# A graph network's edge lists, counts and first projections put in another order on one core

## The chip, the core and the metric

The kernel runs on one core of a Trainium2 chip. Five engines work side by side, each through its own instructions in order, and meet through semaphores: TensorE (PE; matrix products into PSUM), VectorE (DVE), ScalarE (ACT), GpSimd (POOL) and SyncE (SP, which only issues transfers and waits). Transfers are issued by SyncE, ScalarE and GpSimd. The metric is the time of the whole program on the device in microseconds (us).

## The reference

N = 1250 nodes with 768 features, 41,250 edges sorted by target. A normalized copy of x goes through two graph attention layers, the result is added to x, and a transformer block with attention and a mixture of eight experts follows. What the change touches lies before and in the first graph layer:

```python
def _gat_layer(x, W, a_src, a_dst, b, src, dst, n_nodes):
    h = x @ W
    e_src = h @ a_src
    e_dst = h @ a_dst
    e = leaky_relu(e_src[src] + e_dst[dst], 0.2)
    m = segment_max(e, dst, num_segments=n_nodes)
    w = exp(e - m[dst])
    z = segment_sum(w, dst, num_segments=n_nodes)
    alpha = w / z[dst]
    return segment_sum(h[src] * alpha[:, None], dst, num_segments=n_nodes) + b

# first layer, on layernorm(x); loops appended to the edges
h = _gat_layer(x, W1, att_src1, att_dst1, b1, src, dst, n_nodes)
```

The kernel has no gather of h by edge. It turns the edges into a matrix of counts, cnt (how often source j meets target i), and then the layer is dense: weights from outer sums and exponentials, times the counts, times h.

## The kernel before

Nodes are cut into ten tiles of 125 (T = 125, NT = 10). The stretch up to the first aggregation has these steps.

**Edge lists (lines 226 to 390).** The edges are read as 125 rows of 330, and each becomes one number, key = target * 1250 + source (L234). The keys go back to DRAM. VectorE compares the rows' first keys with the nodes (L288), TensorE sums that (L292), and so each pair of nodes knows the row in which its edges begin. Five gathers by GpSimd fetch those rows (kr, L329), VectorE counts in them (`first_edges`, L299) and five more gathers fetch the 128 keys from each pair's first edge on (win, L302). L353 to L366 take the pair's base off, throw out what isn't the pair's and sum what was found; L380 transposes the lists, and L385 to L390 split each into a part of the target and source (pb, jb). If not all edges were found, a slow loop at L413 counts them by another way: `turns` is 0 when all were found, and then it runs no turn.

**Row tiles.** For each tile of x, `spread` takes mean and deviation (L120 to L124), `normal` normalizes the rows (L317, ScalarE), `columns` transposes them into xT (L141, copied by L273), and `project` multiplies a tile with W1 (gw) into h: 12 products, each shown as two matmuls, 24 a tile (L204), then one copy (L207).

**Tables.** GpSimd writes `lane` (128 x 3200) and `upto` (128 x 2500) with iotas (L250, L332).

**Counts (L392 to L407).** In 25 groups VectorE builds one-hot tables, oh in each group (L400) and ohj in every fifth (L397), TensorE makes 25 small products from them (L404), and ScalarE copies the sums into cnt (L406). oh and the PSUM tile pc have two buffers each.

**After the loop at L413.** The diagonal is added (L433), VectorE multiplies W1 with the attention vectors (reps; `attention_vector`, L182), TensorE makes the terms (L194) and es (L473), VectorE the maxima (L480 to L501), and `rest_of_first` (L535) projects the tiles from EARLY on. Weight tiles wt (L517) and h meet in the aggregation (L524).

**What sets the order.** Inside `tc.manual_schedule` the order of the program text is the order of the named engines: TensorE, VectorE and GpSimd from L323 on, TensorE and VectorE in the counts. `tc.keep_in_program_order` does so for single instructions, here the loads and stores of SyncE and ScalarE. All else is ordered by a planner, within a block of code; a loop such as L413 ends a block, and nothing moves past it. A transfer holds one of a few semaphores, and a later one that gets the same semaphore is issued only when the earlier has landed.

Of the kernel before, what the change touches and what calls it, by code (L numbers as in the profile page):

```python
# [10 lines left out]
F32 = mybir.dt.float32  # L11
F16 = mybir.dt.float16
BF16 = mybir.dt.bfloat16
I32 = mybir.dt.int32
# [3 lines left out]
ALU = mybir.AluOpType  # L18
# [9 lines left out]
def gnn_ffn_kernel(  # L28
# [132 lines left out]
    with tc.tile_pool(name="cnt", bufs=1) as cpool:  # L161
# [36 lines left out]

        def project(xT, w, h, psum, tiles):
            for t in tiles:  # L200
                po = psum.tile([T, 2, 512], F32, tag="po", name="ph")
                for s in range(2):
                    for c in range(DC):
                        nc.tensor.matmul(po[:, s, :DH], xT[:, c, t * T:(t + 1) * T],  # L204
                                         w[:, c, s * DH:(s + 1) * DH],
                                         start=(c == 0), stop=(c == DC - 1))
                nc.scalar.copy(h[:, t, :D].rearrange("p (s d) -> p s d", s=2), po[:, :, :DH])  # L207
# [6 lines left out]
        EARLY = 3  # L214
        with tc.tile_pool(name="edge", bufs=1) as ep, \
# [4 lines left out]
            def queue(eng, o, i):  # L220

                for rs in (slice(0, 112), slice(112, T)):
                    tc.keep_in_program_order(eng.dma_start(o[rs], i[rs]))
# [5 lines left out]
            for i, (eng, a) in enumerate(((nc.sync, dst), (nc.scalar, src))):  # L229
                queue(eng, ri[:, i, :], a.rearrange("(p e) -> p e", p=T))  # L230
            tc.keep_in_program_order(nc.scalar.dma_start(keys[E:E + SL].rearrange("(o e) -> o e", o=1), tail))
# [12 lines left out]
            nc.vector.tensor_scalar(pair, pair, 2.0 * N, None, ALU.mult)  # L244
            nodes = ep.tile([T, N], F32, name="nodes")
# [4 lines left out]
            nc.gpsimd.iota(lane, pattern=[[1, P], [0, PG]], base=0, channel_multiplier=0,  # L250
                           allow_small_or_imprecise_dtypes=True)
# [23 lines left out]

            with tc.tile_pool(name="early", bufs=1) as xp:
                xrows = [xp.tile([T, D], F32, name=f"xn{t}") for t in range(NT)]
                krows = [xp.tile([T, EC], F32, name=f"kr{u}") for u in range(NU)]
                queue(nc.scalar, xrows[1], x[T:2 * T, :])
                queue(nc.scalar, rows, key)  # L280
                for t in (0, 2, 3):
                    queue(nc.sync, xrows[t], x[t * T:(t + 1) * T, :])
                tc.keep_in_program_order(nc.sync.dma_start(gw, gW1.rearrange("(c p) f -> p c f", p=P)))
                for t in range(4, NT):
                    queue(nc.sync, xrows[t], x[t * T:(t + 1) * T, :])
# [22 lines left out]
                def spread(t):  # L308
                    stats[t] = ln_root(xrows[t])
# [9 lines left out]
                def columns(t):  # L319
                    transpose_rows(gpt, xrows[t], evict_to(xT, t))  # L320

                fixed = {mybir.EngineType.PE, mybir.EngineType.DVE, mybir.EngineType.Pool}
                with tc.manual_schedule(engines=fixed):  # L323
                    pk = find_rows()
                    spread(0)
                    nc.vector.tensor_scalar(row, pk[:T, :NU], -1.0, None, ALU.add)
                    nc.vector.tensor_scalar(edges, pk[:T, :NU], -1.0, float(EC), ALU.add, ALU.mult)
                    for u in range(NU):
                        nc.gpsimd.indirect_dma_start(  # L329
                            out=krows[u], out_offset=None, in_=rows,  # L330
                            in_offset=bass.IndirectOffsetOnAxis(ap=row[:, u:u + 1], axis=0))
                    nc.gpsimd.iota(upto, pattern=[[1, 2 * NT], [0, 5 * PG]], base=1, channel_multiplier=0,  # L332
                                   allow_small_or_imprecise_dtypes=True)
                    for t in range(1, 4):
                        spread(t)
                        normal(t - 1)
                        columns(t - 1)
                    normal(3)
                    columns(3)

                    for t in range(4, NT):
                        if t < 4 + NU:
                            first_edges(t - 4)
                        spread(t)
                        if t > 4:
                            normal(t - 1)
                        if t % 2 == 0:
                            project(xT, gw, h, gpo, [t // 2 - 2])
                        if t > 4:
                            columns(t - 1)  # L350
                    normal(NT - 1)
                    columns(NT - 1)
                    nc.vector.tensor_tensor(win, win, pair[:, :, None].to_broadcast([T, NU, SL]), ALU.subtract)  # L353

            op = edge.enter_context(tc.tile_pool(name="onehot", bufs=2))
            reps = [every_partition(a, op, "rep", nc.sync) for a in (ga_src1, ga_dst1)]

            wf = win.rearrange("p u s -> p (u s)")
            ge = ep.tile([T, NU * SL], F32, name="ge")
            nc.vector.tensor_scalar(ge, wf, 0.0, None, ALU.is_ge)  # L360
            found = ep.tile([T, 1], F32, name="found")
            nc.vector.scalar_tensor_tensor(ge, wf, 2.0 * N, ge, op0=ALU.is_lt, op1=ALU.mult,
                                           accum_out=found)
            FAR = 1048576.0
            nc.vector.scalar_tensor_tensor(wf, wf, FAR, ge, op0=ALU.add, op1=ALU.mult)
            nc.vector.tensor_scalar(wf, wf, -FAR, None, ALU.add)  # L366
            pf = gpt.tile([P, 4, P], F32, tag="tr", name="psum")
            nc.tensor.matmul(pf[:, 0, 0:1], ones[:T, :P], found, start=True, stop=True)
            good = ep.tile([P, 1], F32, name="good")
            nc.vector.tensor_scalar(good, pf[:, 0, 0:1], float(E), None, ALU.is_equal)  # L370
            turns = ep.tile([1, 1], I32, name="turns")
            nc.vector.tensor_scalar(turns, good[0:1], -float(EC // EB), float(EC // EB), ALU.mult, ALU.add)


            lt = op.tile([P, NP], F32, name="lt", bufs=1)
            for u0 in range(0, NU, 4):
                n = min(4, NU - u0)
                pt = gpt.tile([P, 4, P], F32, tag="tr", name="pl")
                for u in range(u0, u0 + n):
                    nc.tensor.transpose(pt[:, u - u0, :T], win[:, u, :], ident[:T, :T])  # L380
                nc.scalar.copy(lt[:, u0 * T:(u0 + n) * T].rearrange("p (u q) -> p u q", q=T), pt[:, :n, :T])

            jf = op.tile([P, NP], F32, name="jf", bufs=1)
            half = (T - 1) // 2
            nc.vector.tensor_scalar(jf, lt, -float(half), 1.0 / T, ALU.add, ALU.mult)  # L385
            nc.vector.tensor_scalar(jf, jf, 12582912.0, -12582912.0, ALU.add, ALU.add)
            pb = ep.tile([P, NP], BF16, name="pb")
            nc.vector.scalar_tensor_tensor(pb, jf, -float(T), lt, op0=ALU.mult, op1=ALU.add)
            jb = ep.tile([P, NP], BF16, name="jb")
            nc.vector.tensor_scalar(jb, jf, 1.0, good, ALU.add, ALU.mult)  # L390
            ohj = op.tile([P, NP // (5 * PG), 2 * NT, 5 * PG], BF16, name="ohj", bufs=1)
            with tc.manual_schedule(engines={mybir.EngineType.PE, mybir.EngineType.DVE}):  # L392
                for g in range(NP // PG):
                    gs = slice(g * PG, (g + 1) * PG)
                    if g % 5 == 0:
                        js = slice(g * PG, (g + 5) * PG)
                        nc.vector.tensor_tensor(ohj[:, g // 5], jb[:, None, js].to_broadcast([P, 2 * NT, 5 * PG]), upto,  # L397
                                                ALU.is_equal)
                    oh = op.tile([P, P, PG], BF16, tag="oh", name="ohp")
                    nc.vector.tensor_tensor(oh, pb[:, None, gs].to_broadcast([P, P, PG]), lane, ALU.is_equal)  # L400
                    pf = epc.tile([P, 512], F32, tag="pc", name="pc")
                    pc = pf[:, :PG * 2 * NT].rearrange("p (q e) -> p q e", e=2 * NT)
                    for k in range(PG):
                        nc.tensor.matmul(pc[:, k, :], oh[:, :, k], ohj[:, g // 5, :, (g % 5) * PG + k], start=True, stop=True)  # L404
                    c0 = 2 * g * PG
                    nc.scalar.copy(cnt[:, :, c0:c0 + 2 * PG],  # L406
                                   pc[:T].rearrange("p q (i j) -> p j (q i)", i=2))  # L407
# [23 lines left out]
            for t in range(NT):  # L431
                d = cnt[:, t, t * T:(t + 1) * T]
                nc.vector.tensor_tensor(d, d, ident[:T, :T], ALU.add)  # L433
            for i, a in enumerate(reps):
                attention_vector(0, i, gw, a, op, "scr")
# [656 lines left out]
```

## Time and profile before

| | us |
|---|---|
| median of 3 runs (lowest, highest) | 1527.41 (1524.62, 1529.33) |
| the profiled execution | 1522.34 |
| its span | 1520.5 |
| first key gather issued (L329) | 10.54 |
| weights gw landed, first projection starts (L204) | 19.32 |
| lists' transposes (L380) | 52.01 |
| first and last matmul of the counts (L404) | 59.26 to 112.11 |
| diagonal (L433) | 113.20 |
| es copied, maxima begin (L482) | 132.25 |
| first aggregation matmul (L524) | 190.20 |

All the change is in the first 190 us. Busy time of TensorE over the span is 1433.7 us, of VectorE 811.9, of ScalarE 595.6, of GpSimd 418.6. The page counts an engine as busy while an instruction of it is in flight, so a full TensorE may still run at half its clock; the granted clock is a column of its own. To find what a change in one stage is worth, one looks for the engine that ends each wait in that stage.

### The profile page before, as it was taken

The page shows a single profiled execution, that of the slowest core. Times are in us where ns is not written, and L with a number is a line of the kernel's source. Part 1 is how long each engine was busy: PE and PEld are TensorE (multiplying, and loading weights), DVE is VectorE, ACT ScalarE, POOL GpSimd, SP SyncE. Part 2 cuts the span into 40 slices and gives each one's busy share as a digit, 9 for nine tenths or more (in the row PEclk, how much of TensorE's full clock was granted, in tenths as well). Part 3 has the DMA queues.
Part 4 walks back from the last instruction along what each step waited for, and adds up shares of the span by engine and source line. Part 5 has one row for each costly group of instructions (what it writes and reads, how often), then busy time and mean ns, then how long its engine had stood idle before and what let it go on. Part 6 is the DMA issues. An engine that isn't in the chain of part 4 may idle for free.

```text
span 1520.5 us, 15858 instructions
## 1 busy us (share of the span) xinstructions
PE 1433.7 (94%) x5952; PEld 779.0 (51%) x5952; DVE 811.9 (53%) x1311; ACT 595.6 (39%) x924; POOL 418.6 (28%) x276
## 2 busy tenths in 40 slices
PE   6787999999999999999999999999989996899997
PEld 4574555556555555543343343344333664565654
DVE  6688456434036640127778778778787764111111
ACT  4221513205116521136556646646656354221211
POOL 5000000000000010006646646655657222122222
PEclk9758999999999999999999999999999997899999
DMA  7000020010021139920000000000120432855643
GB/s 207 22 2 11 11 73 0 0 32 1 15 88 45 57 100 396 407 86 0 22 1 0 22 1 21 1 22 0 28 75 1 144 119 107 300 172 185 219 153 134
DMA packets 48199, 124.66 MB, mean 82 GB/s; under 512 B 5629, under 2 KB 22207, under 8 KB 48120
## 3 DMA queue, kind: packets, MB, share of 16 engines
q1 hardware_dynamic: 31468, 57.36, 11.5%
q0 software_dynamic: 11968, 56.26, 9.8%
q10 hardware_dynamic: 4684, 9.99, 2.2%
q8 instruction: 48, 0.79, 0.2%
q14 instruction: 31, 0.25, 0.1%
HBM read 70.47 MB, written 57.60 MB: 84 GB/s over the span
## 4 chain that ended last, share of the span: by engine, by line
PE 67%; DVE 9%; issue 7%; ACT 4%; DMA 4%; POOL 1%; POOLq 0%; SPq 0%; ACTq 0%; DVEq 0%
PE pagg L524 13%; PE st L676 8%; PE ph L204 7%; PE pav L720 7%; PE pk L639 5%; PE pv L655 5%; PE phe L1006 5%; PE poe L1015 5%; PE pq L639 4%; DMA xd<-yn,slot 2%; DVE sT L706 2%; PE po L864 2%; ACT sT L679 1%; DVE most L685 1%; PE mb L701 1%
## 5 line engine op out<-in xcount | busy, mean ns | idle before, releaser
L712 POOL TENSOR_TENSOR acc<-acc,sT 125x834 f32<-125x834 f32 (+1 forms) x139 | 273.1, 1964 | 10.9
L524 PE MATMUL pagg<-h,wt 125*125 125x385 f32 (+1 forms) x800 | 263.5, 486 | 0.4 <-DVE wt L517 0.4
L685 DVE TENSOR_TENSOR most<-most,st 125x834 f32<-125x834 f32 (+1 forms) x144 | 147.0, 1021 | 105.5 <-ACT sT L679 102.6
L524 PEld LDWEIGHTS pagg<-h,wt 125*125 125x125 f32 x800 | 147.0, 187 | 104.7 <-DVE wt L517 3.5
L706 DVE TENSOR_TENSOR sT<-sT,mb 125x834 f32<-125x834 f32 (+1 forms) x180 | 174.1, 1015 | 22.6 <-PE mb L701 22.6
L707 ACT ACTIVATE sT<-sT 125x834 f32<-125x834 f32 (+1 forms) x180 | 158.4, 900 | 49.2 <-DVE sT L706 48.8
L679 ACT COPY sT<-st 125x834 f32<-125x834 f32 (+1 forms) x180 | 151.6, 848 | 52.4 <-PE st L676 50.7
L676 PE MATMUL st<-qk 64*125 64x417 f32 (+1 forms) x720 | 164.5, 556 | 3.9 <-DVE most L685 3.8
L720 PE MATMUL pav<-sT,v 125*64 125x417 f32 (+1 forms) x720 | 151.0, 532 | 9.0 <-ACT sT L707 9.0
L617 POOL MEMSET zero<- 128x772 f32 x1 | 0.7, 742 | 530.2 <-PE ptr L141 530.2
L712 POOL TENSOR_TENSOR acc<-sT 125x834 f32<-125x834 f32 (+1 forms) x18 | 35.4, 1965 | 274.6 <-ACT sT L707 274.6
L676 PEld LDWEIGHTS st<-qk 64*125 64x125 f32 x720 | 56.5, 184 | 99.1 <-issue 42.7
L720 PEld LDWEIGHTS pav<-sT,v 125*64 125x64 f32 x720 | 42.5, 136 | 105.7 <-issue 43.9
L1015 PE MATMUL poe<-we,hT 128*128 128x384 f32 x264 | 88.8, 486 | 0.0
L639 PE MATMUL pq<-yT,wqk 128*128 128x417 f32 (+1 forms) x216 | 88.1, 534 | 0.0
L864 PE MATMUL po<-wp,aT 128*125 128x384 f32 x240 | 87.5, 498 | 0.0
L1019 DVE SCALAR_TENSOR_TENSOR sofar<-poe,weight,sofar 128x768 f32<-128x768 f32 x25 | 25.4, 1018 | 114.6 <-PE poe L1015 107.7
L1006 PE MATMUL phe<-xT,we 128*128 128x384 f32 (+1 forms) x288 | 86.6, 460 | 0.0
L639 PE MATMUL pk<-yT,wqk 128*128 128x417 f32 (+1 forms) x216 | 84.0, 526 | 0.0
L204 PE MATMUL ph<-gw,xnT 128*125 128x384 f32 x240 | 81.4, 498 | 0.5 <-DMA gw<-in_L_gnn_W_dram 0.5
L655 PE MATMUL pv<-wv,yT 128*125 128x384 f32 x240 | 79.9, 490 | 1.4 <-issue 1.4
L528 DVE RECIPROCAL rz<-pagg 125x1 f32<-125x1 f32 x20 | 3.3, 166 | 141.5 <-PE pagg L524 141.5
(222 smaller groups left out, 1788.2 us busy)
## 6 DMA issues: line engine op xcount, KB each, us to landing
xd<-zero POOLq DMA_DIRECT2D x8, 3860.0 KB, 15.2
we<-in_L_ffn_W_dram SPq DMA_DIRECT2D x16, 1152.0 KB
xr<-xd SPq DMA_DIRECT2D x25, 386.0 KB
gw<-in_L_gnn_W_dram SPq DMA_DIRECT2D x2, 2304.0 KB
wqk<-in_L_ffn_Wqkv_dram SPq DMA_DIRECT2D x12, 384.0 KB
xres<-in_x_dram SPq DMA_DIRECT2D x10, 375.0 KB
xsd<-xres ACTq DMA_DIRECT2D x10, 375.0 KB
xn<-in_x_dram SPq DMA_DIRECT2D x9, 336.0 KB
```

The costliest lines, as they stand in the source:

```text
L204: nc.tensor.matmul(po[:, s, :DH], xT[:, c, t * T:(t + 1) * T], w[:, c, s * DH:(s + 1) * DH], start=(c == 0), stop=(c == DC - 1))
L524: nc.tensor.matmul(po[:, s, :DH + s], ws[j][:, (d - d0) * T:(d - d0 + 1) * T], h[:, j, s * DH:(s + 1) * DH + s], start=(j == 0), stop=(j = ...
L639: nc.tensor.matmul(pq[:, :w], wqk[:, c, i, :], yT[:, c, c0:c0 + w], start=(c == 0), stop=(c == DC - 1))
L676: nc.tensor.matmul(st[:T, i, :w], self.qk[r, 1, j * T:(j + 1) * T], self.qk[r, 0, self.c0:self.c0 + w], start=True, stop=True)
L679: nc.scalar.copy(s[:, :, :w], st[:T, :, :w])
L685: nc.vector.tensor_tensor(self.most[:, :, :w], prev[:, :, :w], st[:T, :, :w], ALU.max)
L706: nc.vector.tensor_tensor(s[:, :, :w], s[:, :, :w], self.mb[:T, :, :w], ALU.subtract)
L707: nc.scalar.activation(s[:, :, :w], s[:, :, :w], AF.Exp)
L712: nc.gpsimd.tensor_tensor(self.acc[:, :, :w], prev[:, :, :w], s[:, :, :w], ALU.add)
L720: nc.tensor.matmul(self.pav[r, :w], v[:, j, hd0:hd0 + HD], s[:, i, :w], start=(j == 0), stop=(j == NT - 1))
L1006: nc.tensor.matmul(ph[:, :n * P], w1[:, c, f * P:(f + 1) * P], xT[:, c, :n * P], start=(c == 0), stop=(c == DC - 1))
L1015: nc.tensor.matmul(po[:, d, :DH], hT[:, f, s * P:(s + 1) * P], w2[:, f, d * DH:(d + 1) * DH], start=(f == 0), stop=(f == FC - 1))
```

## The change

It moves work rather than taking it away:

- The tables lane and upto are no longer written by GpSimd. GpSimd writes one row table, upto128, and ScalarE copies it out, lane at the start and upto after the columns of tile 3.
- The store of the keys and of their tail, before on ScalarE's queue, is on SyncE's, between the rows of tile 0 and those of tiles 2 and 3.
- The rows of tiles 4 to 9 are loaded straight into h's space, and wait for the last of the five key gathers.
- All five `first_edges` come before the statistics of tile 4. The list steps come ahead of the statistics of tiles 7, 8 and 9.
- Tile 0 is projected before the columns of tile 4, tile 1 behind the lists' transposes, tile 2 one product at a time within the counts (groups 9 to 23, three of four), tiles 3 and 4 behind the counts but before the loop at L413. EARLY goes from 3 to 5, so five tiles are left after es instead of seven.
- Normals and columns of tiles 8 and 9 and the statistics of tile 9 lie within the counts; ohj has two buffers of one fifth each.
- The attention rows (reps) are loaded after the loop and the diagonal instead of before.

```diff
+        def project_steps(xT, w, h, psum, t):
+            po = psum.tile([T, 2, 512], F32, tag="po", name="ph")
+            for s in range(2):
+                for c in range(DC):
+                    nc.tensor.matmul(po[:, s, :DH], xT[:, c, t * T:(t + 1) * T],
+                                     w[:, c, s * DH:(s + 1) * DH],
+                                     start=(c == 0), stop=(c == DC - 1))
+                    if s == 1 and c == DC - 1:
+                        nc.scalar.copy(h[:, t, :D].rearrange("p (s d) -> p s d", s=2), po[:, :, :DH])
+                    yield None
+
         def project(xT, w, h, psum, tiles):
             for t in tiles:
...
+                for _ in project_steps(xT, w, h, psum, t):
+                    pass
...
-        EARLY = 3
+        EARLY = 5
...
-            tc.keep_in_program_order(nc.scalar.dma_start(keys[E:E + SL].rearrange("(o e) -> o e", o=1), tail))
...
+            upto128 = ep.tile([P, P + 1], F32, name="upto128")
+            nc.gpsimd.iota(upto128, pattern=[[1, P + 1]], base=0, channel_multiplier=0,
+                           allow_small_or_imprecise_dtypes=True)
...
-            nc.gpsimd.iota(lane, pattern=[[1, P], [0, PG]], base=0, channel_multiplier=0,
-                           allow_small_or_imprecise_dtypes=True)
...
+                xrows = [xp.tile([T, D], F32, name=f"xn{t}") if t < 4 else h[:, t, :D] for t in range(NT)]
                 krows = [xp.tile([T, EC], F32, name=f"kr{u}") for u in range(NU)]
                 queue(nc.scalar, xrows[1], x[T:2 * T, :])
-                queue(nc.scalar, rows, key)
-                for t in (0, 2, 3):
+                tc.keep_in_program_order(nc.scalar.copy(lane, upto128[:, :P, None].to_broadcast([P, P, PG])))
+                queue(nc.sync, xrows[0], x[0:T, :])
+                queue(nc.sync, rows, key)
+                tc.keep_in_program_order(nc.sync.dma_start(keys[E:E + SL].rearrange("(o e) -> o e", o=1), tail))
+                for t in (2, 3):
                     queue(nc.sync, xrows[t], x[t * T:(t + 1) * T, :])
                 tc.keep_in_program_order(nc.sync.dma_start(gw, gW1.rearrange("(c p) f -> p c f", p=P)))
-                for t in range(4, NT):
-                    queue(nc.sync, xrows[t], x[t * T:(t + 1) * T, :])
...
                     for u in range(NU):
-                        nc.gpsimd.indirect_dma_start(
+                        ins = nc.gpsimd.indirect_dma_start(
                             out=krows[u], out_offset=None, in_=rows,
                             in_offset=bass.IndirectOffsetOnAxis(ap=row[:, u:u + 1], axis=0))
-                    nc.gpsimd.iota(upto, pattern=[[1, 2 * NT], [0, 5 * PG]], base=1, channel_multiplier=0,
-                                   allow_small_or_imprecise_dtypes=True)
+
+                    for t in range(4, NT):
+                        for load in queue(nc.sync, xrows[t], x[t * T:(t + 1) * T, :]):
+                            if t == 4:
+                                tc.add_manual_dep(load.ins, ins.ins.name, mybir.DependencyInfo(
+                                    mybir.DependencyClass.Sync, mybir.DependencyReason.DATA), reason="rows of edges first")
...
                     normal(3)
                     columns(3)
-
-                    for t in range(4, NT):
-                        if t < 4 + NU:
-                            first_edges(t - 4)
+                    tc.keep_in_program_order(nc.scalar.copy(
+                        upto, upto128[:, 1:2 * NT + 1, None].to_broadcast([P, 2 * NT, 5 * PG])))
+                    for u in range(NU):
+                        first_edges(u)
+                    project(xT, gw, h, gpo, [0])
+                    for t in range(4, 7):
                         spread(t)
                         if t > 4:
                             normal(t - 1)
-                        if t % 2 == 0:
-                            project(xT, gw, h, gpo, [t // 2 - 2])
-                        if t > 4:
                             columns(t - 1)
-                    normal(NT - 1)
-                    columns(NT - 1)
+                    normal(6)
+                    columns(6)
+
                     nc.vector.tensor_tensor(win, win, pair[:, :, None].to_broadcast([T, NU, SL]), ALU.subtract)
-
-            op = edge.enter_context(tc.tile_pool(name="onehot", bufs=2))
-            reps = [every_partition(a, op, "rep", nc.sync) for a in (ga_src1, ga_dst1)]
...
+                    nc.vector.scalar_tensor_tensor(wf, wf, FAR, ge, op0=ALU.add, op1=ALU.mult)
+                    nc.vector.tensor_scalar(wf, wf, -FAR, None, ALU.add)
+                    pf = gpt.tile([P, 4, P], F32, tag="tr", name="psum")
+                    nc.tensor.matmul(pf[:, 0, 0:1], ones[:T, :P], found, start=True, stop=True)
+
+                    for u0 in range(0, NU, 4):
+                        n = min(4, NU - u0)
+                        pt = gpt.tile([P, 4, P], F32, tag="tr", name="pl")
...
+                    spread(7)
+                    nc.vector.tensor_scalar(good, pf[:, 0, 0:1], float(E), None, ALU.is_equal)
...
+                    nc.vector.tensor_scalar(jb, jf, 1.0, good, ALU.add, ALU.mult)
+                    spread(8)
+                    normal(7)
+                    project(xT, gw, h, gpo, [1])
+                    columns(7)
+                    more = project_steps(xT, gw, h, gpo, 2)
+                    for g in range(NP // PG):
...
+                        nc.vector.tensor_tensor(oh, pb[:, None, gs].to_broadcast([P, P, PG]), lane, ALU.is_equal)
+                        if g in (2, 3):
+                            normal(g + 6)
+                        if g == 2:
+                            spread(9)
+                        if g in (4, 6):
+                            columns(g // 2 + 6)
+                        if g > 7 and g % 4 != 0:
+                            next(more)
...
+                    for _ in more:
+                        pass
+                    project(xT, gw, h, gpo, range(3, EARLY))
...
             for t in range(NT):
                 d = cnt[:, t, t * T:(t + 1) * T]
                 nc.vector.tensor_tensor(d, d, ident[:T, :T], ALU.add)
+            reps = [every_partition(a, op, "rep", nc.sync) for a in (ga_src1, ga_dst1)]
```

## The prediction

> **What bounds the kernel now.** I first looked at the busy shares: TensorE is busy for 94% of the span, but in the first tenth the granted clock is low. The change touches only the stretch up to the first aggregation matmul at 190.20 us, so I read that stretch in order of time (start, busy us, engine, line, operation, count, idle time before it and who ended it):
>
> ```profile
> 10.54 1.38 POOL L329 DMA_INDIRECT kr<-keys,row  x1 [2.62 <-DVE st L120]
> 18.65 0.56 DVE L299 SCALAR_TENSOR_TENSOR key<-kr,pair,ones 125x330 f32<-125x330 f32 x1 [4.33 <-DMA kr<-keys,row]
> 19.32 10.54 PE L204 MATMUL ph<-gw,xnT 128*125 128x384 f32 x24 [0.51 <-DMA gw<-in_L_gnn_W_dram]
> ...
> 34.83 0.83 DVE L353 TENSOR_TENSOR win<-win,pair 125x640 f32<-125x640 f32 x1 [0.38 <-DMA win<-keys,at]
> ...
> 40.26 7.91 PE L204 MATMUL ph<-gw,xnT 128*125 128x384 f32 x24
> 52.01 0.75 PE L380 MATMUL pl<-ident,win 125*128 125x125 f32 x5
> 59.26 3.64 PE L404 MATMUL pc<-ohj,ohp 128*128 128x20 bf16 x50 [6.49 <-DVE ohp L400]
> ```
>
> The lists (win) are finished by VectorE at 38.4, yet their transposes (L380) run at 52.01: they stand behind the second and third projected tile on TensorE. Counting starts at 59.25 and its last matmul ends at 112.11, 52.85 us later. In that stage VectorE sets the pace: five one-hot tables take 9.54 us, 1.91 each, and every fifth group adds 1.46 for ohj, while TensorE needs 1.82 a group. The windows view (busy us of each engine, then the granted clock) says at what clock:
>
> ```profile
> core 0: us, PE busy (x) PEld busy (x) DVE busy (x) ACT busy (x) POOL busy (x), PEclk, DMA share, GB/s
> 60.00:112.00 52.00, 44.82 (x617) 42.97 (x615) 48.74 (x28) 13.87 (x24) 0.00 (x0) 0.50 0.01 2
> ```
>
> Then comes the guarded loop at L413, which runs no turn. The view of that line and the chain of waits show that it is a meeting of all engines:
>
> ```profile
> L413 SPq EVENT_SEMAPHORE  x12: 28/28/54886, 53.6 to 112.8; - x12
> L413 POOLq EVENT_SEMAPHORE  x12: 42/43/55061, 53.3 to 112.9; - x12
> ```
>
> ```profile
> 112.13 0.48 ACT cnt L406
> 112.61 0.03 DVEq L413
> ...
> 113.20 2.08 DVE cnt L433 x10
> 115.28 6.17 DVE scr L182 x14
> ```
>
> SyncE and GpSimd have nothing to do with the counts, and wait 55 us there until the last count has been copied. VectorE goes through only after ScalarE's last copy. So whatever stands before L413 on TensorE or ScalarE holds VectorE's next work. After it, the diagonal, the attention vectors and terms take 19.0 us up to the terms es (132.2), and from there TensorE is full with seven projected tiles until 190.0. The tenth weight tile wt is ready at 171.4.
>
> **The change, part by part.**
>
> *Lists, up to the first count matmul: before 59.25.* The two tables leave GpSimd. The five-element operation on pair took 2.47 us and ended with the lane table; now begun ends near 6.2 instead of 8.27. The row numbers then wait for x rows and their statistics (1.2 us), and the gather also stood behind the next tile's statistics (1.1 us): first gather about 9.3 instead of 10.54. ScalarE copies instead: its activations cost 0.96 us per 1000 elements plus 0.23 (500 in 0.71, 375 in 0.59 us), so lane 3.3 us and upto 2.6 us. I put both at nothing: lane runs about 4.4 to 7.7, before the first root (9.46 before), and upto while ScalarE waits for rows; without that cover they cost their 3.3 and 2.6. The key store and the tail move to SyncE, where tiles 2, 3 and gw queue behind them; the key is ready at 5.24 and gw was issued only at 8.47, held by earlier transfers, so gw lands near 19.3 again.
>
> Row loads 4 to 9 (twelve DMAs) now wait for the landing of the last key gather, with everything of SyncE behind them. Gathers landed at 18.6, 21.5, 23.7, 25.4, 27.5 while row loads shared the engines. Shifted by 1.25: 17.3 and 19.7; then gw is done, and about 1 us each follows: 22.2 for the last. [...]
>
> Rows 4 then land near 25.3 and rows 6 near 27.2 (0.9 us a tile at some 400 GB/s). VectorE has statistics of tiles 4 to 6 ahead of the lists: 25.4 + 3 x 1.22 + 0.9 = 30.0; the list steps take 3.6 as before: 33.7. The second transpose group needs the buffer that good frees, and good stands behind statistics of tile 7 (1.25): 35.2. TensorE had tile 0 (19.3 to 29.8) and columns 4 to 6 (to 32.9). Tile 1 follows: 35.5 + 7.9 = 43.4, columns 7 1.3: **counting starts at 44.7, that is -14.5**. Of that, 7.9 (tile 2) and 2.6 (columns 8 and 9) are only moved. Bounds: gw landing at 17.5 gives -18; gathers as late as before give -9.2.
>
> *Counts: before 52.85.* VectorE gets statistics of tile 9 and two normals: 1.25 + 0.54 = 1.8 in groups 2 and 3, in its bounding time. Columns 8 and 9 (1.45 each on TensorE): the first hides in those 1.8, the second costs about 1.2. Tile 2 comes as 12 steps of two matmuls. The first matmuls of tile 0, before the clock came up at 24.5, started 0.64 us apart, later 0.33 (7.91/24): a step is 1.3 us at half clock, 0.66 at full. TensorE's room in groups 9 to 24 is 34.9 - 29.1 = 5.8 us; 12 steps need 15.6 or 7.9. So +9.8 or +2.1 and, with the rest, **+13.0 at half clock, +5.8 at full**. [...] The row says 0.50 all through. [...] I take +13.0, and keep +5.8.
>
> *Tiles 3 and 4 behind the counts.* 48 matmuls: 15.7 us at full clock plus 2.2 for about 4.5 us of half clock at first (tile 0 lost 2.63): 17.9. Then ScalarE's copy, 0.8, its turn-count load and the gate: diagonal 19.2 us after the last count, against 1.1 (112.11 to 113.20): **+18.1**. TensorE's idle 9.4 us during the attention vectors looks like cover, but VectorE cannot pass L413 before. Bounds +16 (clock up) and +19.5.
>
> *The attention rows (reps) behind the loop.* They were loaded at 51.5 under the list steps; two DMAs of 384 KB landed 3.8 and 4.4 us after issue. Now SyncE issues them at the gate: 3.9 against the diagonal's 2.1: **+1.8**, the second is hidden behind six products.
>
> *Five tiles instead of seven after es.* 2 x 7.9: **-15.8**; aggregation could begin 42.0 us after es, the tenth wt is there 39.2 after, so none of it is lost.
>
> Sum: -14.5 + 13.0 + 18.1 + 1.8 - 15.8 = **+2.6 us**. The profiled execution took 1522.34 (span 1520.5), so 1524.9; it is 5.1 under the median of the runs, 1527.41. On that scale: **1530.0**.
>
> **Rivals.**
>
> *The clock comes up within the counts* (faster). [...] Against it: the 52 us of counts without a rise. Then -7.2 in the counts and -2.2 behind them: -6.8, 1520.6.
>
> *The gate does not hold VectorE for tiles 3 and 4* (faster). The terms would follow the projection warm, es 25.1 us after the last count against 20.1: +5.0 in place of +19.9, so -12.3, 1515. Against it: the 55 us waits above, and that VectorE's own waits there end with ScalarE's load.
>
> *Late gathers* (slower). Rows 4 to 6 stand behind the last gather's landing, and the list steps behind their statistics on VectorE: each us of that landing is a us of the counts. If it lands at 27.5 as before, +5.3: +7.9, 1535.3. It decides from 24.2 on. For it: gw alone moved 390 to 420 GB/s before the first gather had a byte; against it: five row tiles less in their way.
>
> *It does nothing where it matters*: tile 2, columns, tiles 3 and 4 are moved work, so a sum near zero is the likeliest case itself.
>
> **How the numbers follow.** Likeliest 0.46, its own range 1525 to 1535; clock 0.18; gate 0.12; late gathers 0.24. A measurement can tell about 0.3%, 4.6 us. Faster: 0.15 of clock, 0.12 of gate, 0.03 of the likeliest: 0.30. Slower: 0.20 of late gathers and 0.14 of the likeliest (at 2.6 it is 2 us from that line): 0.34. Same: 0.36. The range takes in the clock rival's and the late gathers' bounds, and leaves out most of the gate's: 1515 to 1540.
>
> **What would show it.** First gather near 9.3, the last landing near 22; L380 near 34 to 35; the first L404 near 44.7, the last ending near 110.6 with granted clock 0.50; 48 matmuls of projection next, and L433 only after their last copy, near 130; a wait for rep ahead of L182; first L524 near 192.8. Wrong if L433 starts within 2 us of the last count, if the clock is 1.0 in the counts, or if counting starts before 41 or after 50.

## The result and the profile after

The changed kernel takes 1530.03 us (median of 20 runs, 1528.06 to 1532.61), the kernel before 1527.20 on the same chip: a ratio of 1.0023 (95% interval 1.0015 to 1.0031), 2.8 us slower by the medians. A second set of runs gave 1.0026 (1.0018 to 1.0035). The loss is small but clear of the noise; it is inside the 0.3% that the prediction called no change, and 1530.0 had been predicted.

The profiled execution took 1530.82 us (span 1529.1). First the timeline of the changed kernel up to the first count (start, busy us, engine, line, operation, and the idle time before it with who ended it):

```profile
9.84 1.38 POOL L349 DMA_INDIRECT kr<-keys,row  x1 [6.51 <-DVE row L346]
20.34 0.56 DVE L319 SCALAR_TENSOR_TENSOR key<-kr,pair,ones 125x330 f32<-125x330 f32 x1 [6.01 <-DMA kr<-keys,row]
23.58 9.83 PE L204 MATMUL ph<-gw,xnT 128*125 128x384 f32 x24 [4.76 <-DMA gw<-in_L_gnn_W_dram]
...
36.53 0.82 DVE L377 TENSOR_TENSOR win<-win,pair 125x640 f32<-125x640 f32 x1 [1.34 <-DMA win<-keys,at]
41.39 1.30 PE L390 MATMUL pl<-ident,win 125*128 125x125 f32 x5 [0.85 <-DVE good L393]
42.49 8.84 PE L204 MATMUL ph<-gw,xnT 128*125 128x384 f32 x24
51.80 3.46 PE L425 MATMUL pc<-ohj,ohp 128*128 128x20 bf16 x50
```

The transposes of the lists (L390) moved from 52.0 to 41.4, as two projected tiles left their way, but every landing in front of them came later than I had put it. The chain that ended last, in order of time (start, us, what), names two of these landings:

```profile
11.52 10.88 DMA kr<-keys,row
27.97 8.48 DMA win<-keys,at
42.69 8.63 PE ph L204 x24
```

The second key gather is 10.88 us under way, and the last gather of the lists, issued at 27.97, is 8.48 us under way. In the kernel before, the last one took 3.4: its list step, at 34.83, had waited for it, and it was issued here:

```profile
31.38 1.20 POOL L302 DMA_INDIRECT win<-keys,at  x1 [0.90 <-DVE at L301]
```

The counts now hold tile 2. The windows view (window, its length, busy us of each engine, granted clock):

```profile
core 0: us, PE busy (x) PEld busy (x) DVE busy (x) ACT busy (x) POOL busy (x), PEclk, DMA share, GB/s
54.00:116.00 62.00, 59.57 (x631) 49.71 (x630) 49.14 (x34) 18.38 (x32) 0.00 (x0) 0.50 0.01 1
```

TensorE shows busy in 59.57 of 62.00 us, at a granted clock of 0.50. Then come tiles 3 and 4, and what waits for them; first the timeline, then the line of the guarded loop, now L437:

```profile
115.97 17.44 PE L204 MATMUL ph<-gw,xnT 128*125 128x384 f32 x48
...
133.45 0.80 ACT L208 COPY h<-ph 125x768 f32<-125x768 f32 x1 [6.94 <-PE ph L204]
134.52 2.09 DVE L457 TENSOR_TENSOR cnt<-cnt,ident 125x125 uint16<-125x125 uint16 x10 [21.21 <-ACT h L208]
136.52 0.96 DVE L182 SCALAR_TENSOR_TENSOR scr<-gw,rep 128x768 f32<-128x768 f32 x1
```

```profile
L437 DVEq EVENT_SEMAPHORE  x13: 21/50/13314, 113.4 to 134.2; - x13
L437 SPq EVENT_SEMAPHORE  x12: 27/28/67314, 44.3 to 134.1; - x12
```

VectorE stands idle 21.21 us before the diagonal, until ScalarE's last copy of h. SyncE waits 67.3 us at the loop. The attention products (L182) follow the diagonal at once: they did not wait for rep.

Of the kernel before and of the changed kernel there is a second profile each. Stage by stage, in us ("maxima" is the first L482, L507 after the change; "the rest" is all from the first aggregation matmul on):

| stage | before | before, again | after | after, again |
|---|---|---|---|---|
| start to first count | 59.3 | 63.0 | 51.8 | 52.5 |
| counts | 52.9 | 52.9 | 64.3 | 64.3 |
| last count to diagonal | 1.1 | 1.1 | 18.4 | 19.1 |
| diagonal to maxima | 19.1 | 19.0 | 18.4 | 18.7 |
| maxima to first aggregation | 58.0 | 58.0 | 43.7 | 42.5 |
| the rest | 1330.3 | 1332.6 | 1332.5 | 1331.8 |
| span | 1520.5 | 1526.5 | 1529.1 | 1528.9 |

### The profile page after: what moved, and what is told of

The parts are those of the page before. It is cut to its first block, busy times and chain, and to the rows that moved or that the text cites. A ratio compares the mean times of both kernels' runs of the same rounds, so it can differ in the third digit from the quotient of the medians.

```text
span 1529.1 us, 15845 instructions
## 1 busy us (share of the span) xinstructions
PE 1445.8 (95%) x5952; PEld 784.9 (51%) x5952; DVE 810.0 (53%) x1311; ACT 602.5 (39%) x927; POOL 411.3 (27%) x275
## 3 DMA queue, kind: packets, MB, share of 16 engines
q1 hardware_dynamic: 31624, 57.53, 11.5%
## 4 chain that ended last, share of the span: by engine, by line
PE 71%; DVE 9%; issue 7%; DMA 6%; ACT 4%; POOL 1%; SPq 0%; POOLq 0%; ACTq 0%; DVEq 0%
PE pagg L549 12%; PE ph L204 10%; PE st L701 8%; PE pav L745 7%; PE pk L664 5%; PE pv L680 5%; PE phe L1031 5%; PE poe L1040 5%; PE pq L664 4%; PE pc L425 2%; DVE sT L731 2%; DMA xd<-yn,slot 2%; PE po L889 2%; ACT sT L704 1%; DVE most L710 1%
## 5 line engine op out<-in xcount | busy, mean ns | idle before, releaser
L204 PE MATMUL ph<-gw,xnT 128*125 128x384 f32 x240 | 96.9, 559 | 4.8 <-DMA gw<-in_L_gnn_W_dram 4.8
L745 PEld LDWEIGHTS pav<-sT,v 125*64 125x64 f32 x720 | 42.5, 136 | 105.6 <-issue 43.9
L204 PE MATMUL ph<-gw,x1T 128*125 128x384 f32 x240 | 78.8, 488 | 0.0
## 6 DMA issues: line engine op xcount, KB each, us to landing
xd<-zero POOLq DMA_DIRECT2D x8, 3860.0 KB, 42.5
```

The costliest lines, as they stand in the source:

```text
L745: nc.tensor.matmul(self.pav[r, :w], v[:, j, hd0:hd0 + HD], s[:, i, :w], start=(j == 0), stop=(j == NT - 1))
```

## The experiments

All are edits of the changed kernel unless another is named. Each is compared with runs of the kernel before beside it, whose medians were 1524.9 to 1526.8.

**Tiles 3 and 4 behind the loop.** Is it the place in front of the loop that makes them cost, or the work?

```diff
-                    project(xT, gw, h, gpo, range(3, EARLY))
...
             reps = [every_partition(a, op, "rep", nc.sync) for a in (ga_src1, ga_dst1)]
+            project(xT, gw, h, gpo, range(3, EARLY))
```

> Tiles 3 and 4 are projected behind the guarded loop instead of before it; all work stays. If the loop's meeting of all engines is what made them cost: the diagonal starts about 1.1 us after the last count instead of 18.4, TensorE projects from about 2 to 19 us after it while VectorE works on the attention vectors, the terms follow at full clock, and es comes about 27 us after the last count instead of 37: 10 us faster than the changed kernel (some 1520, range 1516 to 1523), faster than the kernel before too. If TensorE's own time for the two tiles is the bound, or VectorE is slowed: within 3 us of the changed kernel.

Measured: 1520.81, ratio 0.9950 (0.9932 to 0.9968). Its timeline:

```profile
116.28 2.08 DVE L456 TENSOR_TENSOR cnt<-cnt,ident 125x125 uint16<-125x125 uint16 x10 [3.92 <-ACT cnt L427]
117.11 18.50 PE L204 MATMUL ph<-gw,xnT 128*125 128x384 f32 x48 [1.93 <-issue]
...
135.54 4.39 PE L194 MATMUL pe<-xnT,wa 128*32 128x417 f32 x36
```

The same 48 matmuls, behind the loop in the text, no longer hold VectorE: the diagonal starts 1.1 us after the last count, and the attention vectors run under the projection. From the last count to the maxima it is 27.3 us instead of 36.7: the 17.3 us in front of the loop are gone, and 7.9 come back between the diagonal and the maxima (26.2 instead of 18.4). The gate, that is the loop holding VectorE for the work in front of it, is shown.

**EARLY = 3**: tiles 3 and 4 where they were before the change, after es.

```diff
-        EARLY = 5
+        EARLY = 3
```

> EARLY is 3 again, the only edit: tiles 3 and 4 are projected after es with the other five. By the sum of the prediction: the diagonal 1.1 us after the last count (-17.3), the stretch from es to the first aggregation +15 to +16 longer: 1.5 to 3 us faster than the changed kernel. If VectorE's work covered the two tiles behind the counts: 14 us or more slower.

Measured: 1528.28, ratio 1.0005 (0.9995 to 1.0016), 1.8 us below the changed kernel by the medians, as the sum had it. In the profile the diagonal is back at 1.1 us after the last count, and the maxima to the first aggregation take 59.2 instead of 43.7: two tiles in front of the loop cost about what they save behind es.

**Tile 2 out of the counts**, projected behind them instead.

```diff
-                        if g > 7 and g % 4 != 0:
-                            next(more)
...
-                    for _ in more:
-                        pass
-                    project(xT, gw, h, gpo, range(3, EARLY))
+                    project(xT, gw, h, gpo, range(2, EARLY))
```

> Tile 2 leaves the counts and is projected behind them with tiles 3 and 4, before the loop; all work stays. If each step in the counts costs its 1.3 us at half clock and TensorE had no room: the counts go from 64.3 to about 54.5 us, the stretch behind them from 18.4 to 26.2: 2 us faster. If the steps lay in room that TensorE had: the counts stay, and it is 8 us slower.

Measured: 1527.51, ratio 1.0003 (0.9991 to 1.0015). The windows view of its counts:

```profile
core 0: us, PE busy (x) PEld busy (x) DVE busy (x) ACT busy (x) POOL busy (x), PEclk, DMA share, GB/s
54.00:107.00 53.00, 45.44 (x610) 43.76 (x608) 49.03 (x34) 17.75 (x31) 0.00 (x0) 0.51 0.01 2
```

The counts take 55.1 us instead of 64.3. So the twelve steps cost 9.2, and what else was moved in (statistics, normals, columns) costs 2.3. The same tile costs 7.5 behind the counts (25.9 instead of 18.4 up to the diagonal): in the counts, at a clock of 0.51, it is not cheaper, but somewhat dearer.

**Row loads 4 to 9 do not wait for the last key gather.**

```diff
-                        for load in queue(nc.sync, xrows[t], x[t * T:(t + 1) * T, :]):
-                            if t == 4:
-                                tc.add_manual_dep(load.ins, ins.ins.name, ...
+                        queue(nc.sync, xrows[t], x[t * T:(t + 1) * T, :])
```

> Row loads 4 to 9 no longer wait for the last key gather. If that wait held the lists (rows 4 to 6 land late, and the list steps stand behind their statistics on VectorE): rows are there when the last gather lands, the list steps start near 33 instead of 36.5, 3 us faster, though the last gather lands later (28 to 29 instead of 25). If the row loads slow the gathers by more than that: list steps at 37 or later, and no gain or up to 3 us slower.

Measured: 1530.14, ratio 1.0027 (1.0017 to 1.0036). Its timeline:

```profile
29.24 0.56 DVE L319 SCALAR_TENSOR_TENSOR key<-kr,pair,ones 125x330 f32<-125x330 f32 x1 [0.61 <-DMA kr<-keys,row]
...
36.88 0.83 DVE L374 TENSOR_TENSOR win<-win,pair 125x640 f32<-125x640 f32 x1 [2.37 <-DMA win<-keys,at]
```

The last gather landed 4.1 us later (29.2 instead of 25.1), the first list step came within 0.4 us of where it was. So the wait is not what holds the lists back, and it neither gains nor loses.

**gw behind rows 4 to 6**, so after the key gathers.

```diff
-                tc.keep_in_program_order(nc.sync.dma_start(gw, gW1.rearrange("(c p) f -> p c f", p=P)))
...
+                            if t == 6:
+                                tc.keep_in_program_order(nc.sync.dma_start(gw, gW1.rearrange("(c p) f -> p c f", p=P)))
```

> The load of gw queued behind rows 4 to 6, so after the last key gather has landed; all else as in the change. Theory 'gw in flight holds the gathers back': the first gather lands about 3.4 us after its issue (near 13 to 14 instead of 20.3), the last near 19 instead of 25; gw then lands near 29, tile 0 is projected from 29 to 39, the list transposes stand behind it and counting begins near 52 as before: time within 2 us of the change's 1530.0. Rival 'the gathers take about 2 us each by themselves': the last lands at 22 or later, gw at 32, counting begins at 54 to 55 and the time is 1532 to 1534.

Measured: 1536.87, ratio 1.0076 (1.0059 to 1.0093). Its timeline:

```profile
9.31 1.38 POOL L348 DMA_INDIRECT kr<-keys,row  x1 [5.98 <-DVE row L345]
13.94 0.59 DVE L318 SCALAR_TENSOR_TENSOR key<-kr,pair,ones 125x330 f32<-125x330 f32 x1
...
20.10 0.56 DVE L318 SCALAR_TENSOR_TENSOR key<-kr,pair,ones 125x330 f32<-125x330 f32 x1 [0.66 <-DMA kr<-keys,row]
...
30.96 0.82 DVE L378 TENSOR_TENSOR win<-win,pair 125x640 f32<-125x640 f32 x1 [0.78 <-DMA win<-keys,at]
35.67 1.00 PE L204 MATMUL ph<-gw,xnT 128*125 128x384 f32 x1 [17.21 <-DMA gw<-in_L_gnn_W_dram]
```

The gathers bear the theory out: the first is counted at most 4.6 us after its issue (10.5 in the changed kernel), the last at 20.1 instead of 25.1, and the list steps begin 5.6 us earlier. The queues show where the time goes. From 10 to 14 us, with three gathers issued, only the queue of the plain loads (q1) moved anything in the changed kernel (first line: packets, MB, share of the 16 engines); with gw held back, the gathers' queue (q0) moved 0.25 MB (the other two):

```profile
q1 hardware_dynamic: 434, 1.24, 92.5%
...
q0 software_dynamic: 231, 0.25, 25.3%
q1 hardware_dynamic: 112, 0.26, 16.4%
```

The time misses the theory: gw, issued at 22.55 beside row loads and gathers, landed at 35.7 and not near 29, tile 0 stands ahead of the transposes, and counting began at 59.8. What the gathers won, gw lost, and more.

**The tables by GpSimd again.**

```diff
+            nc.gpsimd.iota(lane, pattern=[[1, P], [0, PG]], ...)
...
-                tc.keep_in_program_order(nc.scalar.copy(lane, upto128[:, :P, None].to_broadcast([P, P, PG])))
...
+                    nc.gpsimd.iota(upto, pattern=[[1, 2 * NT], [0, 5 * PG]], ...)
...
-                    tc.keep_in_program_order(nc.scalar.copy(
-                        upto, upto128[:, 1:2 * NT + 1, None].to_broadcast([P, 2 * NT, 5 * PG])))
```

> The two tables written by GpSimd again, all else as in the change. Theory (the begun-earlier tables bring nothing, the row numbers wait for something else): first gather issued at most 0.7 us later (10.5 instead of 9.84), first count matmul within 1 us of 51.8, time 1529 to 1531. Rival (GpSimd's tables hold VectorE as in the kernel before, where the five-element operation took 2.47 us): begun ends near 8.3, the lists stand 2 us later and the time is about 1532.

Measured: 1530.58, ratio 1.0035 (1.0025 to 1.0046), so no different from the change within the intervals. Row numbers came 0.8 us later (10.18), the first gather at 10.63, the first count at 51.90. Its timeline has one thing more:

```profile
20.46 9.92 PE L204 MATMUL ph<-gw,xnT 128*125 128x384 f32 x24 [0.82 <-DMA gw<-in_L_gnn_W_dram]
...
22.70 0.55 DVE L317 SCALAR_TENSOR_TENSOR key<-kr,pair,ones 125x330 f32<-125x330 f32 x1
...
36.24 0.82 DVE L375 TENSOR_TENSOR win<-win,pair 125x640 f32<-125x640 f32 x1 [4.05 <-DMA win<-keys,at]
```

Here gw landed 3 us earlier and the last key was counted 2.4 us earlier, and the list steps began where they had: VectorE was done with the row statistics and waited 4.05 us for the last list gather, which had been issued at 27.07 and was 9.1 us under way, beside the row loads.

**Tiles 2 and 3 behind the loop, none in the counts, six after es**: the two findings together.

```diff
-        EARLY = 5
+        EARLY = 4
...
-                        if g > 7 and g % 4 != 0:
-                            next(more)
...
-                    for _ in more:
-                        pass
-                    project(xT, gw, h, gpo, range(3, EARLY))
...
             reps = [every_partition(a, op, "rep", nc.sync) for a in (ga_src1, ga_dst1)]
+            project(xT, gw, h, gpo, range(2, EARLY))
```

> Tiles 2 and 3 projected behind the loop, nothing of a projection within the counts or between them and the loop, and six tiles after es. If the counts only lose the steps' time (64.3 to about 55) and the two tiles hide under the diagonal and the attention vectors as tiles 3 and 4 did when they stood behind the loop, then from that run (1520.8): counts -9.2, one tile more after es +7.9, so about 1519.5. If the steps within the counts had been hidden at half clock after all, the counts stay near 64 and the time is 1528 to 1529.

Measured: 1517.01, ratio 0.9947 (0.9931 to 0.9963). It is below both kernels; against the one with tiles 3 and 4 behind the loop the intervals overlap. Its timeline behind the counts:

```profile
109.06 17.81 PE L204 MATMUL ph<-gw,xnT 128*125 128x384 f32 x48 [1.94 <-issue]
126.81 4.39 PE L194 MATMUL pe<-xnT,wa 128*32 128x417 f32 x36
```

Against the second profile of the kernel before it is: lists -11.0, counts +2.3, diagonal to maxima +6.6, maxima to aggregation -6.6, together -8.7 us.

**The kernel before, once more.**

> The kernel before, unchanged, once more: what two executions of the same kernel differ by, stage by stage. If the stage behind the first layer was low by chance in the first profile (736.9 us from the first matmul pq to the first poe, 737.8 to 739.3 in the other kernels), it is near 738 to 739 here and the first aggregation matmul still at 189 to 193; if instead the change costs those 2 us there, it is 736.9 again.

Measured: 1527.19, ratio to the other runs of the same kernel 1.001 (1.000 to 1.002). Its timeline:

```profile
23.23 10.37 PE L204 MATMUL ph<-gw,xnT 128*125 128x384 f32 x24 [4.41 <-DMA gw<-in_L_gnn_W_dram]
...
55.75 0.75 PE L380 MATMUL pl<-ident,win 125*128 125x125 f32 x5
62.99 3.17 PE L404 MATMUL pc<-ohj,ohp 128*128 128x20 bf16 x43 [6.49 <-DVE ohp L400]
```

The same program, with gw landed at 23.2 instead of 19.3 and counting begun 3.7 us later. The first aggregation was at 193.9, a little outside what I expected. From the first pq to the first poe it took 739.2, so the 2.3 us by which the first profile was shorter there are not the change's doing. Why gw lands at 19.3 in one execution and at 23.2 in another is not shown.

**The changed kernel, once more.**

> The changed kernel once more: 1530 within 1 us; counts 64.3 us and diagonal 18.4 us after the last count as in its first profile. What can differ between executions is the landing of gw (19.3 or 23 us seen so far): if it lands near 20 here, the first count matmul still starts at 51 to 52, since the last gather of the lists under the row loads sets it.

Measured: 1530.9, ratio 1.0026. Counts 64.3, diagonal 19.1 after the last count, counting begun at 52.5. gw landed at 22.7, so the case of an early gw did not come up in it.

**Rows 7 to 9 behind the lists**, on the kernel with tiles 2 and 3 behind the loop.

```diff
-                    nc.gpsimd.indirect_dma_start(
+                    return nc.gpsimd.indirect_dma_start(
                         out=win[:, u, :], ...
...
-                    for t in range(4, NT):
+                    for t in range(4, 7):
...
                     for u in range(NU):
-                        first_edges(u)
+                        ins = first_edges(u)
+                    for t in range(7, NT):
+                        for load in queue(nc.sync, xrows[t], x[t * T:(t + 1) * T, :]):
+                            if t == 7:
+                                tc.add_manual_dep(load.ins, ins.ins.name, ...
```

> As the kernel with tiles 2 and 3 behind the loop (1517.0), and rows 7 to 9 wait for the landing of the last gather of the lists (win); rows 4 to 6 still wait for the last key gather. Theory (the win gathers are held back by the row loads, 8.5 us for the last one instead of 3.4): the last one lands near 33 instead of 36.3, the first list step starts there or where the statistics of tile 6 end (34 to 35), counting begins 1.5 to 3 us earlier than 52.0, the time is 1514 to 1516. Rival (rows 7 to 9 then come too late for the statistics of tile 7, ahead of the list's split on VectorE, and for the columns of tile 8 within the counts): counting begins no earlier, 1517 to 1519.

Measured: 1517.34, ratio 0.9934 (0.9920 to 0.9948); no different. Its timeline:

```profile
32.62 1.02 DVE L120 BATCH_NORM_STATS2 st<-h 125x6 f32<-125x384 f32 x2
...
34.71 0.83 DVE L382 TENSOR_TENSOR win<-win,pair 125x640 f32<-125x640 f32 x1
```

VectorE no longer waits for the list gather, but its own statistics of tiles 4 to 6 end at the same place, and counting begins at 50.2 instead of 52.0. A kernel without this edit, the next one, has 50.1, and VectorE did not wait there either: the two limits lie within what executions differ by, and the time decides neither theory. The landings recorded in the traces do decide one part. The last list gather landed 4.5 us after its issue here (28.16 to 32.67), and 6.4 to 9.1 us after it in the nine profiles where rows 4 to 9 are loaded beside it and gw lies in its old place. So the row loads do hold it back; it brings no time, since VectorE's own work ends as late.

**Tile 2 alone behind the loop**, seven after es (EARLY = 3 in the kernel with two there).

> As the kernel with tiles 2 and 3 behind the loop (1517.0), with tile 2 alone there and seven tiles after es. If the attention vectors cover one tile (TensorE idle for 9.4 us there in the kernel before; a tile from cold is 10.1 us), the terms start some 8 us earlier and one tile of 7.9 is added behind: within 1 us of 1517. If there is no such cover, it is 7.9 us slower, 1525.

Measured: 1520.22, ratio 0.9953 (0.9939 to 0.9968), beside 0.9934 for the kernel above against the same runs. The 1517 within 1 us that was expected is missed by 3: its six runs (1519.15 to 1521.23) all lie above the six of the kernel above (1516.18 to 1518.05). By the profile, diagonal to maxima is 18.5 us instead of 25.6, and maxima to aggregation 59.1 instead of 51.4, so the stretch that was moved comes out even within 0.8 us. One tile is covered by the attention vectors, and a second one is paid where it stands or where it came from. Of the 3.0 us between these two profiles 2.4 lie behind the first aggregation matmul, in code that the two kernels share; their cause is open.

## Why the prediction was right, and where it was wrong

The time was right, and of the five terms of its sum three hold, one was mis-sized and one was wrong. One of the prediction's own signs of being wrong came true: counting started after 50, at 51.8 and 52.5.

**Counts, +13.0: right (+11.5).** The price of a step at half clock was put at 9.8 for twelve and is 9.2 by the run without them; the moved statistics and columns cost 2.3 instead of 3.0. I had taken it that the clock of the counts before, 0.50 with TensorE busy for 44.82 of 52.00 us, would hold with the steps among them, and kept the 5.8 of a full clock beside it. It held: 59.57 busy us of 62.00 at 0.50. The clock was 1.00 when counting began, and dropped at 54.6 though TensorE shows busy for all of 51 to 55 us; it came up at 119.5, 3.5 us after pure projection began:

```profile
118.00:119.00 1.00, 1.00 (x3) 0.66 (x2) 0.00 (x0) 0.00 (x0) 0.00 (x0) 0.50 0.00 0
119.00:120.00 1.00, 1.00 (x3) 0.45 (x3) 0.00 (x0) 0.00 (x0) 0.00 (x0) 0.77 0.00 0
```

The rival of a clock that comes up in the counts, given 0.18, falls with it. What brings the clock up, and what takes it down, is not shown: these 62 us of a TensorE that shows busy did not bring it up. The sum of this term slips a little: 1.8, 1.2 and 9.8 make 12.8, and at full clock 5.1, not 5.8.

**Tiles 3 and 4 behind the counts, +18.1: right (+17.3)**, and so is its reason, the gate: in the run with them behind the loop the diagonal is back at 1.1 us after the last count. The rival that the gate does not hold VectorE falls.

**Five tiles after es, -15.8: nearly (-14.3, and -15.5 in the second pair of profiles).** Aggregation began 43.7 and 42.5 us after the maxima, against 42.0 forecast; in the first of these the clock dropped to one half from 153.6 to 157.0.

**The attention rows, +1.8: wrong (nothing; the stage got 0.7 shorter).** The step that failed is "now SyncE issues them at the gate". The text has the loads behind the loop, and I held that nothing moves past it. For these two loads that does not hold, nor are they issued after the loop and the diagonal: the trace of the changed kernel has both on SyncE in front of its first branch at the loop (the third line, from the loop's own view), put there by the planner:

```profile
L175 SPq DMA_DIRECT2D rep<-in_L_gnn_att_src_dram x1: 356/356/356, 42.4 to 42.4; - x1
L175 SPq DMA_DIRECT2D rep<-in_L_gnn_att_dst_dram x1: 1142/1142/1142, 42.8 to 42.8; - x1
...
L437 SPq COMPARE_BRANCH  x3: 38/38/49, 44.0 to 134.3; - x3
```

**Lists, -14.5: mis-sized.** Counting began at 51.8 instead of 44.7: -7.5 against the first profile of before, -11.2 against its second. Its start held: the first gather went out at 9.84 (9.3 forecast), and the tables copied by ScalarE cost nothing: behind each copy ScalarE still waited for VectorE (1.32 and 8.65 us), and with GpSimd's tables the first count came no earlier. The earlier begun gave only part of what I had it give: row numbers came at 9.36, as in the kernel before (9.35), since they stand behind the statistics of tile 0, whose rows were there only at 8.2; what came off is that the gather no longer stood behind the next tile's statistics. Three figures of the working failed, and a fourth thing was left out.

1. "gw lands near 19.3 again". In twelve profiles of kernels that load gw in this place it landed between 22.7 and 24.1 ten times, at 19.3 and 20.5 twice, and the kernel before itself shows both. I had taken the execution in front of me for the rule. The working timed the last gathers by an early gw ("then gw is done, and about 1 us each follows"); with gw until 23.6 the last was counted at 25.1, not 22.2. The sum slips here as well: 21.5 less 1.25 is 20.2, not 19.7, and three more at 1 us make 23.2. This is the late-gathers rival in part: its point of decision, 24.2, was passed.
2. "0.9 us a tile at some 400 GB/s" for rows 4 to 6. That rate was one that gw had reached (390 to 420 GB/s by the prediction). While the changed kernel's row loads run (25 to 35 us) the windows view has 226 GB/s, and the statistics of rows 4, 5 and 6 start at 28.8, 31.5 and 33.2: some 2 us a tile. VectorE was through with them at 35.2 instead of 30.0.
3. The lists' own gathers I had not looked at: the last took 8.5 us under these row loads, where 3.4 had been the figure without. It ended 1.3 us after VectorE's other work.
4. Tile 1 was put at 7.9 us, at full clock. The clock had dropped to one half at 37.5 and came back at 44.4, so the tile took 8.84 us (10.25 in the second profile).

The two windows behind points 2 and 4:

```profile
25.00:35.00 10.00, 9.28 (x29) 5.17 (x27) 5.02 (x19) 2.00 (x5) 3.55 (x3) 1.00 0.94 226
...
38.00:44.00 6.00, 4.66 (x16) 3.61 (x17) 4.04 (x11) 2.79 (x8) 0.00 (x0) 0.50 0.09 28
```

The first gather was timed by the row of the kernel before, where it was issued at 10.54 and counted at 18.65, 8.1 us later. In direction that was right: it was counted 10.5 us after its issue with gw in flight, and at most 4.6 after it with gw held back. With gw in flight the gathers' queue moved nothing from 10 to 14 us; what held them is not shown.

**Why the total came out all the same.** Against the second profile of before, the terms are off by +3.3 (lists), -1.5, -0.8, -2.4 (rows of attention), +1.5 and -0.1: together nothing. That they cancel is luck; nothing in the working made one offset another. Against the first profile the list stage is off by 7.1 and the part behind the aggregation by 2.3; that profile was 6 us shorter than the second, and I had corrected its distance to the median by adding 5.1 at the end, without asking in which stage it lay. Against the second profile 3.7 of it lay in the stage that I was costing.

That tile 2 and the others are only moved, so that the sum lies near zero, also holds: the 14.3 us less behind es and what the earlier lists gave were paid again in the counts and in front of the loop.

## What to carry to other kernels

The loop with a run-time count was here a meeting of all engines though it ran no turn (SyncE waited 67.3 us at it): ask of work next to such a loop on which side it stands, because the same two projected tiles cost 17.3 us in front and 7.9 behind, where they run beside the diagonal and the attention vectors. TensorE at half clock had less room than its idle time suggested: it was busy for 45.44 of 53.00 us without the twelve steps of a tile, and they, some 15.6 us at half clock by the prediction's figures, added 9.2 us to the counts, where the same tile behind them adds 7.5. Such a tile is better moved to where the engine idles for want of another, as one tile behind the loop did. And before a stage is costed from one profile, take a second of the same kernel: what differs between the two is a first measure of the error in the numbers read from either.

## What the runs showed of the hardware

- The same load of 2304 KB landed at 19.3 or at 23.2 us in two executions of one program, and in the second counting began 3.7 us later; the cause is open.
- GpSimd's gathers (125 rows of 330 keys, or of 128) depend on what else is in flight: the first counted at most 4.6 us after its issue with little beside it and 10.5 under the large load; for the last gather of the lists 3.4 us without row loads (both profiles of the kernel before), 6.4 to 9.1 with those of six tiles (nine profiles) and 4.5 with three of the six held back.
- TensorE's granted clock averaged 0.50 over 62 us in which it shows busy for 59.57, with twelve steps of the projection among the small products, and rose 3.5 us after the projection stood alone (115.97 to 119.5); what sets it is not shown.
